# Start of each image in a two-layer Mamba and FFN kernel: order of the loads, engine of the column copies, queue of the first inputs

## The chip, the core and the metric

The kernel runs on one core of one Trainium2 chip. The time is that of the device, in microseconds; for the kernel before it is the median of three runs. The core has five engines that this text names: TensorE (PE in the profile, PEld its weight loads), VectorE (DVE), ScalarE (ACT), GpSimd (POOL) and SyncE (SP), which only issues transfers. Each engine works through its own instructions in order.

## The reference

The input x is two images of 96 channels and 128 by 128 pixels, fp32. Two layers are applied.

```python
x = x + L0_conv(ln_c(x))        # four Mamba scans, see below
t = tokens(x); t = t + ffn0(ln_t(t)); x = image(t)
x = x + conv3x3(ln_c(x))        # 3x3, 96 to 96 channels
t = tokens(x); t = t + ffn1(ln_t(t)); x = image(t)
```

`ln_c` is layer norm over the 96 channels of a pixel. `L0_conv` runs a Mamba block over four orders of the 16,384 pixels: by rows, by rows backwards, by columns, by columns backwards. Each block projects 96 to 2 x 192 channels, takes a causal convolution of four taps and SiLU, forms dt, B and C of 16 states, and scans:

```python
h = exp(dt * A) * h + dt * B * u      # 192 channels x 16 states, one step a pixel
y = sum_s(h * C) + D * u;  y = y * silu(z);  out = y @ outp_w.T
```

The four results are put back in image order, joined and projected to 96 channels. The FFN rounds its operands to an 8-bit float and its sums to fp16.

## The kernel before

An image is held in SBUF as one tile `acc` of 96 partitions by 16,384 pixels. Ahead of the images the constants are loaded (L51, helper `const`), and a block of preparation (L78 to L105) loads six weight tensors and forms four tables from them: `amat` (L81, L82), `dmat` (L88), `inx`, which merges the input projection with the convolution's taps (L95), and `gmat`, eight small matmuls and copies (L104, L105). Then for each of the two images three functions run one after another.

`normalize` (L149) reads the image in eight blocks of 2,048 pixels (L147; for the second image seven of them were read during the first image's FFN), takes the layer norm of 32 tiles of 512 pixels (L110 to L124), and stores the result to DRAM twice: by rows as `xnr` (L165) and by columns as `xnc`. For the second, eight staging tiles `stg` of 2,048 pixels (768 KB, three buffers) are filled from the strided view of `xn`, one half by VectorE and one half by ScalarE (L173), and each is stored (L177).

`mamba` (L179) handles the orders in two pairs: rows and columns forwards (pi = 0), then both backwards. A step is one tile of 512 pixels of a pair; there are 64 steps an image. A step's 384 channels lie in three groups of 128, and for each group the 16 states are scanned two at a time, so a step is 24 units, and an image 1,536. In a unit ScalarE makes the decay (L353), GpSimd multiplies B's broadcast rows (L345), VectorE scans (L357) and multiplies with C's rows (L445), and TensorE sums over the states (L361). Ahead of a step stands its prologue: it loads the normalized tile by rows (`xa`) and by columns (`xb`) (L218 for the first step of a pair, after two memsets of the edge at L217; L220 for the others), takes the convolution as matmuls (L204) for the groups in the order 1, 0, 2, with ScalarE emptying PSUM (L231), spreads the mixed group 1 over the partitions with two transfers (`xc<-mix`, L248), applies SiLU (L251), and makes the rows of B, C and dt (L258 to L305). The rows go to DRAM (`bcd`, L269) and are read back broadcast over the partitions (`row`, L341).

`ffn_and_conv` does the rest of the image, and stores it.

What sets the order: all five engines run in the order in which the program is written (`in_order`, L138). `together` (L126) interleaves generators: in each turn every stream makes one step, and stream r starts at turn r, so that layer norm's 32 tiles stand as a pipeline of five stages. A prologue's pieces carry a place (`at` in `prologue`), counted in units, at which they are issued; the first prologue of an image is issued at once. All transfers are issued by SP, in the written order; a transfer also waits for the eighth one before it, since eight semaphores are taken in turn. Pools are laid one behind another in SBUF and are freed as a stack, so the first tile of a new pool waits for those that lay in the same place.

Of the kernel before, what the change touches and what calls it, by code (L numbers as in the profile page):

```python
# [10 lines left out]
F32 = mybir.dt.float32  # L11
# [5 lines left out]
PSUM = bass.MemoryType.PSUM  # L17
# [24 lines left out]
def tile_metaformer(ctx: ExitStack, tc: tile.TileContext, a: dict, out: bass.AP):  # L42
    nc = tc.nc

    cpool = ctx.enter_context(tc.tile_pool(name="const", bufs=1))
    accp = ctx.enter_context(tc.tile_pool(name="accp", bufs=1))
    dpool = ctx.enter_context(tc.tile_pool(name="dram", bufs=2, space=DRAM))

    def const(name, shape):
        t = cpool.tile(list(shape), F32, name=name)  # L50
        nc.sync.dma_start(t, a[name])  # L51
        return t
# [7 lines left out]
    minus_one = cpool.tile([128, 1], F32, name="minus_one")  # L60
    nc.vector.memset(minus_one, -1.0)
    ident = const("ident", (128, 128))
    center = cpool.tile([C, C], F32, name="center")
    nc.vector.tensor_scalar_add(center, ident[0:C, 0:C], -1.0 / C)
    inz = const("inz", (C, 4, DI))
# [9 lines left out]
    dmat = cpool.tile([128, 2, NG, 128], F32, name="dmat")  # L75
    gmat = cpool.tile([128, 2, NG + 1, C], F32, name="gmat")
    inx = cpool.tile([C, 4, 4, DI], F32, name="inx")
    with tc.tile_pool(name="prep", bufs=1) as pp, tc.tile_pool(name="prep_ps", bufs=2, space=PSUM) as pps:  # L78
        alog = pp.tile([128, 2, NG, S], F32, name="alog")
        nc.sync.dma_start(alog, a["alog"])  # L80
        nc.scalar.activation(alog, alog, AF.Exp)  # L81
        nc.vector.tensor_scalar_mul(amat, alog, -1.0)  # L82

        dskip = pp.tile([128, 2, NG], F32, name="dskip")
        nc.sync.dma_start(dskip, a["dskip"])
        for pi in range(2):
            for g in range(NG):
                nc.vector.tensor_scalar_mul(dmat[:, pi, g, :], ident, dskip[:, pi, g : g + 1])  # L88

        inxw = pp.tile([C, 4, DI], F32, name="inxw")  # L90
        nc.sync.dma_start(inxw, a["inx"])
        taps = pp.tile([C, 4, 4, DI], F32, name="taps")
        nc.sync.dma_start(taps, a["taps"].broadcast_to((C, 4, 4, DI)))
        for d in range(4):
            nc.vector.tensor_tensor(inx[:, d], taps[:, d], inxw[:, d, None, :].broadcast_to((C, 4, DI)), ALU.mult)  # L95
        outx = pp.tile([C, 2, NG + 1, 128], F32, name="outx")
        nc.sync.dma_start(outx, a["outx"])
        fusew = pp.tile([C, 4, C], F32, name="fusew")
        nc.sync.dma_start(fusew, a["fusew"])
        for pi, pair in enumerate(PAIRS):  # L100

            for g in range(NG + 1):
                ps = pps.tile([128, C], F32, name="ps")
                nc.tensor.matmul(ps, outx[:, pi, g, :], fusew[:, pair[g // 2], :], start=True, stop=True)  # L104
                nc.vector.tensor_copy(gmat[:, pi, g, :], ps)  # L105

    def layernorm(x, eps, dst, wp, psp, bufs=2, **cast):

        xm = psp.tile([C, T], F32, name="xm", bufs=bufs)
        nc.tensor.matmul(xm, center, x, start=True, stop=True)  # L110
        yield
        sq = wp.tile([C, T], F32, name="sq")
        nc.scalar.activation(sq, xm, AF.Square)  # L113
        yield
        v = psp.tile([C, T], F32, name="v")
        nc.tensor.matmul(v, mean_w, sq, start=True, stop=True)  # L116
        yield
        rs = wp.tile([C, T], F32, name="rs")
        nc.scalar.activation(rs, v, AF.Ln, bias=eps)  # L119
        nc.scalar.activation(rs, rs, AF.Exp, scale=-0.5)  # L120
        yield
        if len(dst.shape) == 3:
            xm, rs = (t.rearrange("c (h w) -> c h w", w=W) for t in (xm, rs))
        nc.vector.tensor_tensor(dst, xm, rs, ALU.mult, **cast)  # L124

    def together(*streams):  # L126

        turn = 0
        streams, done = list(streams), object()
        while streams:  # L130
            left = []
            for at, g in streams:
                if turn < at or next(g, done) is not done:
                    left.append((at, g))
            streams = left
            turn += 1
# [6 lines left out]
    blk = 4 * T  # L143

    def read(b, acc, j):

        nc.sync.dma_start(acc[:, bass.ts(j, blk)], a["x"][b, :, bass.ts(j, blk)])  # L147

    def normalize(b, acc, xnr, xnc):  # L149

        with ExitStack() as st:
            pool = lambda n, bufs, **kw: st.enter_context(tc.tile_pool(name=n, bufs=bufs, **kw))
            full, wp, psp = pool("n1", 1), pool("n2", 3), pool("n_ps", 3, space=PSUM)
            in_order(st)
            nc.scalar.preload_act_table_set("natural_log_exp_and_others")
            xn = full.tile([C, L], F32, name="xn")
            for j in range(L // blk if b == 0 else 1):
                read(b, acc, j if b == 0 else L // blk - 1)

            def one(r):  # L160
                sl = bass.ts(r, T)
                yield from layernorm(acc[:, sl], eps_c[0:C, 0:1], xn[:, sl], wp, psp, 5)
                if (r + 1) % 4 == 0:
                    sl = bass.ts(r // 4, blk)
                    nc.sync.dma_start(xnr[:, sl], xn[:, sl])  # L165

            together(*((r, one(r)) for r in range(NT)))
            cols = xn.rearrange("c (h w) -> c w h", w=W)
            for j in range(L // blk):
                stg = wp.tile([C, blk], F32, name="stg")  # L170
                half = blk // W // 2
                for i, eng in enumerate((nc.vector.tensor_copy, nc.scalar.copy)):
                    eng(  # L173
                        stg[:, i * half * W : (i + 1) * half * W].rearrange("c (w h) -> c w h", h=W),
                        cols[:, j * 2 * half + i * half : j * 2 * half + (i + 1) * half, :],
                    )
                nc.sync.dma_start(xnc[:, bass.ts(j, blk)], stg)  # L177

    def mamba(acc, xnr, xnc):  # L179

        with ExitStack() as st:
            pool = lambda n, bufs, **kw: st.enter_context(tc.tile_pool(name=n, bufs=bufs, **kw))
            io, one, two, gen = pool("io", 2), pool("one", 1), pool("two", 2), pool("gen", 4)
            ps_w, ps_y, ps_m = (pool(n, k, space=PSUM) for n, k in (("ps_w", 3), ("ps_y", 1), ("ps_m", 1)))
            rows_d = pool("rows_d", 3, space=DRAM)

# [20 lines left out]
            def prologue(pi, i, d):  # L207

                rev = pi == 1
                lo = L - (i + 1) * T if rev else i * T  # L210
                src = []

                def load():
                    for n, dram in (("xa", xnr), ("xb", xnc)):
                        t = io.tile([C, T + 3], F32, name=n)
                        if i == 0:
                            nc.gpsimd.memset(t[:, T : T + 3] if rev else t[:, 0:3], 0.0)  # L217
                            nc.sync.dma_start(t[:, 0:T] if rev else t[:, 3 : T + 3], dram[:, lo : lo + T])  # L218
# [20 lines left out]
                    nc.scalar.copy(mixed("sz") if g == 1 else d["sz"][:, g, :], d["ps"])  # L239

                def mixed(name):
                    d["mix", name] = one.tile([128, T], F32, name="mix")
                    return d["mix", name]

                def mix(name):
# [227 lines left out]
            for k in range(total + 6):  # L473
# [22 lines left out]
    def ffn_and_conv(b, acc):  # L496

        with ExitStack() as st:
# [32 lines left out]
            def ffn(n, r):  # L531
# [64 lines left out]
    acc = accp.tile([C, L], F32, name="acc")  # L596
# [77 lines left out]
```

## Time and profile before

| | us |
|---|---|
| median of three runs | 12174.19 |
| the three runs | 12160.50 to 12199.53 |
| the profiled execution | 12198.56 |
| its span | 12196.8 |
| busy VectorE, GpSimd | 10962.5, 9908.7 |
| busy TensorE, ScalarE | 10601.0, 8585.5 |

The profile is that of one execution. Its page gives, by engine, the busy time and the busy share in 40 equal slices of the span, and groups of instructions by line, with their mean duration in nanoseconds and the idle time of the engine just before them. A line of the timeline has the start and the duration in us, the engine, the line of the code, the operation, what it writes and reads, the number of instructions that were merged into the line, and in brackets how long the engine had been idle and what released it. A table of stretches gives the busy time of PE, PEld, DVE, ACT and POOL in each, with the number of instructions, then TensorE's granted clock, the share of the transfer engines and GB/s. "To landing" is the time from a transfer's issue to its last byte.

### The profile page before, as it was taken

Reading aid. Unit: us, or ns where it says so; the run is one execution under the profiler, and the core shown is the slowest. Engines: PE = TensorE matmul, PEld = TensorE weight load, DVE = VectorE, ACT = ScalarE, POOL = GpSimd, SP = SyncE. Lnnn points to the kernel's source line nnn. Section 1 sums busy time; section 2 is a strip of 40 time slices with the busy share of each in tenths; the row PEclk is TensorE's granted clock in tenths of the full one; section 3 lists DMA queues with packets and bytes.
Section 4 is the critical chain, followed back from the end, with each engine's and each line's share of the span. In section 5 each row is a group of like instructions: output and inputs, shape, how many; then the busy total and the mean of one; then the engine's idle time right before and its main releaser. Section 6 shows DMA issues by size and latency. Waiting matters only on the chain. (4 is left out here: it accounts for less than half of the span.)

```text
span 12196.8 us, 95712 instructions
## 1 busy us (share of the span) xinstructions
PE 10601.0 (87%) x24208; PEld 4012.8 (33%) x24208; DVE 10962.5 (90%) x10624; ACT 8585.5 (70%) x15110; POOL 9908.7 (81%) x5336
## 2 busy tenths in 40 slices
PE   7888888888888888888978888888888888888889
PEld 2333333333333333333323333333333333333333
DVE  6999999999999999995469999999999999999954
ACT  6777777777777777775577777777777777777655
POOL 5998999999998989891159989999989999988811
PEclk9999999999999999999989999999999999999999
DMA  7887888788877878781068888888878878878700
GB/s 250 309 319 302 307 319 313 309 318 312 318 310 306 319 305 310 308 317 47 26 242 307 308 317 312 314 318 313 313 307 308 321 308 316 314 305 309 304 32 13
DMA packets 539169, 3417.07 MB, mean 280 GB/s; under 512 B 67276, under 2 KB 68396, under 8 KB 140696
## 3 DMA queue, kind: packets, MB, share of 16 engines
q1 hardware_dynamic: 538616, 3410.94, 72.9%
q8 instruction: 195, 3.19, 0.1%
q14 instruction: 358, 2.93, 0.1%
HBM read 3289.04 MB, written 54.53 MB: 274 GB/s over the span
## 5 line engine op out<-in xcount | busy, mean ns | idle before, releaser
L345 POOL TENSOR_TENSOR row<-dtu,row 128x2048 f32<-128x2048 f32 x1536 | 6949.9, 4525 | 820.8 <-DMA row<-bcd 658.5
L357 DVE TENSOR_TENSOR_SCAN da<-da,row 128x512 f32<-128x512 f32 x5632 | 6650.2, 1215 | 509.8 <-ACT da L353 187.3
L361 PE MATMUL y<-row,ident 128*128 128x512 f32 x12288 | 5957.9, 618 | 1130.5 <-DVE row L445 1125.7
L353 ACT ACTIVATE da<-dt,amat 128x512 f32<-128x512 f32 x6144 | 4250.4, 692 | 278.7 <-DVE row L357 92.0
L361 PEld LDWEIGHTS y<-row,ident 128*128 128x128 f32 x12288 | 2268.5, 194 | 4643.0 <-issue 2296.4
L445 DVE TENSOR_TENSOR row<-da,row 128x1024 f32<-128x1024 f32 x2816 | 3395.8, 1206 | 1.0 <-DMA row<-bcd 0.9
L446 ACT COPY hst<-da 128x2 f32<-128x2 f32 x2816 | 434.7, 154 | 1423.8 <-DVE row L445 1412.4
L204 PE MATMUL misc<-xa,inx 96*64 96x512 f32 (+1 forms) x2048 | 963.6, 614 | 131.3 <-DMA xa<-xnr 108.0
L204 PE MATMUL misc<-xb,inx 96*64 96x512 f32 (+1 forms) x2048 | 962.3, 613 | 1.9 <-ACT xc L231 1.6
L568 POOL TENSOR_TENSOR acc<-acc,y 96x512 f32<-96x512 f32 x128 | 147.4, 1152 | 987.1 <-DVE y L567 987.1
L357 DVE TENSOR_TENSOR_SCAN row<-da,row 128x512 f32<-128x512 f32 x512 | 616.9, 1205 | 0.0
L364 POOL TENSOR_TENSOR row<-row,row 128x1024 f32<-128x1024 f32 x256 | 602.8, 2355 | 7.1 <-DVE row L357 6.1
L580 PE MATMUL pc<-pad,kw 96*96 96x512 f32 x1152 | 566.7, 593 | 0.0
L452 PE MATMUL y<-xc,dmat 128*128 128x512 f32 x768 | 428.9, 640 | 145.2 <-DVE sz L368 145.2
L295 POOL TENSOR_TENSOR q<-e,q 128x512 f32<-128x512 f32 x384 | 487.5, 1270 | 71.5 <-ACT q L292 71.5
L204 PEld LDWEIGHTS misc<-xa,inx 96*64 96x64 f32 (+1 forms) x2048 | 329.7, 166 | 650.6 <-issue 444.9
L231 ACT ACTIVATE xc<-misc,convb 128x512 f32<-128x512 f32 x256 | 175.8, 687 | 519.7 <-PE misc L204 519.7
L301 POOL TENSOR_TENSOR dt<-dt,ln 128x512 f32<-128x512 f32 x384 | 487.1, 1269 | 30.1
L298 POOL TENSOR_TENSOR ln<-ln,q 128x512 f32<-128x512 f32 x384 | 487.2, 1269 | 20.1
L305 POOL TENSOR_TENSOR dtu<-dt,xc 128x512 f32<-128x512 f32 x384 | 487.1, 1269 | 10.2
L378 PE MATMUL misc<-sz,gmat 128*96 128x512 f32 x1024 | 483.6, 594 | 0.0
L124 DVE TENSOR_TENSOR xq<-xm,rs 96x512 fp8e5<-96x512 f32 x128 | 87.9, 687 | 388.0 <-ACT rs L120 387.9
(81 smaller groups left out, 9340.4 us busy)
## 6 DMA issues: line engine op xcount, KB each, us to landing
row<-bcd SPq DMA_DIRECT2D x3072, 1024.0 KB, 7.1
xc<-mix SPq DMA_DIRECT2D x256, 128.0 KB, 5.3
sz<-mix SPq DMA_DIRECT2D x256, 128.0 KB, 5.4
xa<-xnr SPq DMA_DIRECT2D x124, 193.1 KB, 5.2
xb<-xnc SPq DMA_DIRECT2D x124, 193.1 KB, 5.5
bcd<-rows SPq DMA_DIRECT2D x128, 128.0 KB, 6.7
acc<-in_x_dram SPq DMA_DIRECT2D x16, 768.0 KB, 8.6
xnr<-xn SPq DMA_DIRECT2D x16, 768.0 KB, 4.3
```

The lines of the kernel that those rows point to most:

```text
L204: nc.tensor.matmul(ps[rows, :], w(PAIRS[pi][d], k, lo, hi), src[d][:, k : k + T], **se)
L295: nc.gpsimd.tensor_tensor(d["q"], d["e"], d["q"], ALU.subtract)
L298: nc.gpsimd.tensor_tensor(d["ln"], d["ln"], d["q"], ALU.add)
L301: nc.gpsimd.tensor_tensor(d["dt"][g], d["dt"][g], d["ln"], ALU.add)
L305: nc.gpsimd.tensor_tensor(dtu, d["dt"][g], d["xc"][:, g, :], ALU.mult)
L345: nc.gpsimd.tensor_tensor(b, d["dtu"][g][:, None, :].broadcast_to((128, 4, T)), b, ALU.mult)
L353: nc.scalar.activation(da[:, j, :], d["dt"][g], AF.Exp, scale=amat[:, pi, g, s + j : s + j + 1])
L357: nc.vector.tensor_tensor_scan(h[:, j, :], da[:, j, :], b[:, j, :], 0.0, ALU.mult, ALU.add)
L361: nc.tensor.matmul(y, ident, c[:, j, :], start=False, stop=s + j == S - 1)
L364: nc.gpsimd.tensor_tensor(c, h, c, ALU.mult)
L445: nc.vector.tensor_tensor(c, h, c, ALU.mult)
L580: nc.tensor.matmul(pc, kw[:, t, :], rows, start=t == 0, stop=t == 8)
```

## The change

Three things are done.

First, the eight reads of the first image are written right behind the load of `ident`, ahead of the other constants and the weights. The preparation becomes a generator `prep` that is one more stream of `together` in the first image's layer norm. Its six loads are issued in turn 0; in turn 18 it forms `amat`, in the two turns after that `dmat`, in four more `inx`, and then a product of `gmat` a turn, copied in the next. Its PSUM pool has one buffer for two, layer norm's `v` two for three.

Second, the columns are copied by VectorE alone, in 16 parts of eight columns (1,024 pixels, 384 KB) with three buffers, in a pool of their own that is opened after layer norm; each part is stored by itself.

Third, the first two inputs of the forward pair are issued on GpSimd's queue, each behind its memset, for SP's. The backward pair's stay on SP. The pools of `normalize` and `mamba` are laid out in another order: layer norm's scratch first, then `xn`; `io` (xa, xb), `gen`, `one`, a pool of its own for `mix`, `two`.

```diff
+    acc = accp.tile([C, L], F32, name="acc")
+    blk = 4 * T
+    def read(b, acc, j):
+        nc.sync.dma_start(acc[:, bass.ts(j, blk)], a["x"][b, :, bass.ts(j, blk)])
+    for j in range(L // blk):
+        read(0, acc, j)
     center = cpool.tile([C, C], F32, name="center")
...
-    with tc.tile_pool(name="prep", bufs=1) as pp, tc.tile_pool(name="prep_ps", bufs=2, space=PSUM) as pps:
-        alog = pp.tile([128, 2, NG, S], F32, name="alog")
-        nc.sync.dma_start(alog, a["alog"])
+    def prep(st):
+        pp = st.enter_context(tc.tile_pool(name="prep", bufs=1))
+        pps = st.enter_context(tc.tile_pool(name="prep_ps", bufs=1, space=PSUM))
...
+        alog, dskip = load("alog", (128, 2, NG, S)), load("dskip", (128, 2, NG))
+        outx, fusew = load("outx", (C, 2, NG + 1, 128)), load("fusew", (C, 4, C))
+        inxw, taps = load("inx", (C, 4, DI)), load("taps", (C, 4, 4, DI), spread=True)
+        for _ in range(18):
+            yield
         nc.scalar.activation(alog, alog, AF.Exp)
         nc.vector.tensor_scalar_mul(amat, alog, -1.0)
...
         for pi in range(2):
+            yield
             for g in range(NG):
                 nc.vector.tensor_scalar_mul(dmat[:, pi, g, :], ident, dskip[:, pi, g : g + 1])
...
         for d in range(4):
+            yield
             nc.vector.tensor_tensor(inx[:, d], taps[:, d], inxw[:, d, None, :].broadcast_to((C, 4, DI)), ALU.mult)
...
                 nc.tensor.matmul(ps, outx[:, pi, g, :], fusew[:, pair[g // 2], :], start=True, stop=True)
+                yield
                 nc.vector.tensor_copy(gmat[:, pi, g, :], ps)
...
-            full, wp, psp = pool("n1", 1), pool("n2", 3), pool("n_ps", 3, space=PSUM)
+            wp, psp = pool("n2", 3), pool("n_ps", 2, space=PSUM)
             in_order(st)
             nc.scalar.preload_act_table_set("natural_log_exp_and_others")
+            full = pool("n1", 1)
             xn = full.tile([C, L], F32, name="xn")
-            for j in range(L // blk if b == 0 else 1):
-                read(b, acc, j if b == 0 else L // blk - 1)
+            if b > 0:
+                read(b, acc, L // blk - 1)
...
-            together(*((r, one(r)) for r in range(NT)))
+            streams = [(r, one(r)) for r in range(NT)]
+            with ExitStack() as weights:
+                together(*streams, *([(0, prep(weights))] if b == 0 else []))
+            stg = pool("n3", 3)
             cols = xn.rearrange("c (h w) -> c w h", w=W)
-            for j in range(L // blk):
-                stg = wp.tile([C, blk], F32, name="stg")
...
+            part = 8
+            for j in range(W // part):
+                t = stg.tile([C, part, W], F32, name="stg")
+                nc.vector.tensor_copy(t, cols[:, bass.ts(j, part), :])
+                nc.sync.dma_start(xnc[:, bass.ts(j, part * W)], t.rearrange("c w h -> c (w h)"))
...
-            io, one, two, gen = pool("io", 2), pool("one", 1), pool("two", 2), pool("gen", 4)
+            io, gen, one, mixp, two = (pool(*p) for p in (("io", 2), ("gen", 4), ("one", 1), ("mixp", 1), ("two", 2)))
...
                             nc.gpsimd.memset(t[:, T : T + 3] if rev else t[:, 0:3], 0.0)
-                            nc.sync.dma_start(t[:, 0:T] if rev else t[:, 3 : T + 3], dram[:, lo : lo + T])
+                            queue = nc.sync if rev else nc.gpsimd
+                            queue.dma_start(t[:, 0:T] if rev else t[:, 3 : T + 3], dram[:, lo : lo + T])
...
-                    d["mix", name] = one.tile([128, T], F32, name="mix")
+                    d["mix", name] = mixp.tile([128, T], F32, name="mix")
```

More of the change, by code (lines that the diff above doesn't have):

```diff
@@ L77, in tile_metaformer, with load @@
     inx = cpool.tile([C, 4, 4, DI], F32, name="inx")
-    with tc.tile_pool(name="prep", bufs=1) as pp, tc.tile_pool(name="prep_ps", bufs=2, space=PSUM) as pps:
-        alog = pp.tile([128, 2, NG, S], F32, name="alog")
-        nc.sync.dma_start(alog, a["alog"])
+    def prep(st):
+        pp = st.enter_context(tc.tile_pool(name="prep", bufs=1))
+        pps = st.enter_context(tc.tile_pool(name="prep_ps", bufs=1, space=PSUM))
+        def load(name, shape, **kw):
+            t = pp.tile(list(shape), F32, name=name)
+            nc.sync.dma_start(t, a[name].broadcast_to(shape) if kw else a[name])
+            return t
+        alog, dskip = load("alog", (128, 2, NG, S)), load("dskip", (128, 2, NG))
[3 more added lines that the diff above has]
+            yield
         nc.scalar.activation(alog, alog, AF.Exp)
         nc.vector.tensor_scalar_mul(amat, alog, -1.0)
-        dskip = pp.tile([128, 2, NG], F32, name="dskip")
-        nc.sync.dma_start(dskip, a["dskip"])
         for pi in range(2):
+            yield
             for g in range(NG):
                 nc.vector.tensor_scalar_mul(dmat[:, pi, g, :], ident, dskip[:, pi, g : g + 1])
[L90 to L93, printed above, removed]
         for d in range(4):
+            yield
             nc.vector.tensor_tensor(inx[:, d], taps[:, d], inxw[:, d, None, :].broadcast_to((C, 4, DI)), ALU.mult)
[L96 to L99, printed above, removed]
         for pi, pair in enumerate(PAIRS):
@@ L141, in in_order @@
         st.enter_context(tc.manual_schedule(engines={et.Activation, et.DVE, et.Pool, et.PE, et.SP}))
-    blk = 4 * T
-    def read(b, acc, j):
-        nc.sync.dma_start(acc[:, bass.ts(j, blk)], a["x"][b, :, bass.ts(j, blk)])
     def normalize(b, acc, xnr, xnc):
@@ L165, in one @@
                     nc.sync.dma_start(xnr[:, sl], xn[:, sl])
-            together(*((r, one(r)) for r in range(NT)))
+            streams = [(r, one(r)) for r in range(NT)]
+            with ExitStack() as weights:
+                together(*streams, *([(0, prep(weights))] if b == 0 else []))
+            stg = pool("n3", 3)
             cols = xn.rearrange("c (h w) -> c w h", w=W)
-            for j in range(L // blk):
-                stg = wp.tile([C, blk], F32, name="stg")
[L171 to L177, printed above, removed]
+            part = 8
[3 more added lines that the diff above has]
+                nc.sync.dma_start(xnc[:, bass.ts(j, part * W)], t.rearrange("c w h -> c (w h)"))
     def mamba(acc, xnr, xnc):
@@ L594, in ffn_and_conv @@
                 together(*((at, f(r - lag)) for lag, at, f in stages if 0 <= r - lag < NT))
-    acc = accp.tile([C, L], F32, name="acc")
     for b in range(NB):
```

## The prediction, written before the result was known

> **What bounds the kernel now.** I read the page first, then a table of four long stretches, then the timeline of the two places that the change touches.
>
> ```profile
> DVE   6999999999999999995469999999999999999954
> ...
> L357 DVE TENSOR_TENSOR_SCAN da<-da,row 128x512 f32<-128x512 f32 x5632 | 6650.2, 1215 | 509.8 <-ACT da L353 187.3
> ```
> ```profile
> 3000.00:4000.00 1000.00, 878.05 (x1979) 330.56 (x1978) 963.93 (x870) 724.90 (x1284) 908.81 (x489) 0.98 0.81 312
> ```
> In the scan loop VectorE (third busy figure) works 964 of 1000 us. The change leaves that loop's instructions alone: the built programs hold the same ones in the same order on every engine. So the only time at stake lies where VectorE is not yet scanning: the first slice (6 of 10) and the same place in image 2, just after the 4 and 5. The loop hands any earlier start on to the end, since each image is serial: normalize, mamba, ffn.
>
> ```profile
> 6.77 8.79 SPq L147 DMA_DIRECT2D acc<-in_x_dram  x8
> ...
> 20.82 3.73 PE L110 MATMUL xm<-acc,center 96*96 96x512 f32 x4 [0.35 <-DVE gmat L105]
> 22.88 0.59 ACT L113 ACTIVATE sq<-xm 96x512 f32<-96x512 f32 x1 [16.01 <-PE xm L110]
> ```
> Timeline of the start: layer norm's first matmul comes at 20.82, released by the last weight product (gmat); the image is asked for only at 6.77.
>
> ```profile
> 80.38 0.69 DVE L124 TENSOR_TENSOR xn<-xm,rs 96x512 f32<-96x512 f32 x1 [0.61 <-ACT rs L120]
> 81.10 5.58 ACT L173 COPY stg<-xn 96x1024 f32<-96x1024 f32 x3 [0.75 <-DVE xn L124]
> 81.11 2.90 DVE L173 COPY stg<-xn 96x1024 f32<-96x1024 f32 x3
> ...
> 88.36 1.02 DVE L173 COPY stg<-xn 96x1024 f32<-96x1024 f32 x1 [4.35 <-DMA xnc<-stg]
> 98.57 1.92 ACT L173 COPY stg<-xn 96x1024 f32<-96x1024 f32 x1 [0.63 <-DMA xnc<-stg]
> 100.55 0.10 POOL L217 MEMSET xa<- 96x3 f32 x1 [100.09 <-ACT stg L173]
> 100.87 1.27 SPq L218 DMA_DIRECT2D xa<-xnr  x1
> 102.19 1.80 SPq L218 DMA_DIRECT2D xb<-xnc  x1
> 107.38 1.09 PE L204 MATMUL misc<-xa,inx 96*64 96x512 f32 x1 [28.41 <-DMA xa<-xnr]
> 113.88 1.19 SPq L248 DMA_DIRECT2D xc<-mix  x2
> 122.83 1.28 ACT L251 ACT_TABLE_LOAD   x1
> 151.40 3.61 DVE L357 TENSOR_TENSOR_SCAN da<-da,row 128x512 f32<-128x512 f32 x3 [51.78 <-POOL row L345]
> ```
> From layer norm to the first scan everything is in series. Layer norm ends at 81.07 (call such an end E), column copies end at 100.5, the first inputs xa, xb arrive at 107.4, three convolutions fill 15.4 us, SiLU's table load starts at 122.83 (E+41.8), the first scan 28.6 later. Image 2: E is 6166.67, the table load 6208.65 (E+42.0).
>
> ```profile
> L173 ACT COPY stg<-xn x8: 1915/1922/1936, 81.1 to 98.6; 96x1024 f32<-96x1024 f32 x8
> L173 DVE COPY stg<-xn x8: 1022/1028/1036, 81.1 to 98.6; 96x1024 f32<-96x1024 f32 x8
> ...
> DMA to landing us min/median/max: 5.2/5.5/6.7
> ```
> The view of tile stg: the copies wait for their stores. Their starts (91.02, 93.49, 96.02, 98.57) stand 2.5 us apart, 768 KB each: some 310 GB/s, so the transfers set the pace and a copy has slack.
>
> [...]
>
> **Part 1, image ahead of weights.** The eight reads move from place 14 on SP's queue to place 2, so from 6.77 to about 1.2. A 288 KB read (inz) landed in 3.1 us at that hour; 480 KB more at the start's 250 GB/s is 1.9: the first block lands at about 1.2+5.1 = 6.3. center is ready at 2.9. The first xm thus comes at 6.3, not 20.82: -14.5. Later blocks (3.1 us each) outrun four tiles of 1.72. Bounds: -16 (4.8) to -12 (8.8).
>
> What moves on SP: inz to fuseb and the six prep loads go behind the reads, and each issue waits for the transfer eight before it. The reads end near 28, taps (7.9 us in its row) lands near 39. The first taps product stands in turn 21, at 6.3+5.4+18x1.717 = 42.6: hidden, with 4 us to spare. The first three xnr stores queue behind taps until about 31 and catch up by layer norm's end; nobody reads them before.
>
> **Part 2, products between tiles.** A tile takes 1.717 us, all of it ScalarE (0.57+0.67+0.63, overlapping a little). alog's exp is ScalarE's: +0.28. VectorE has 1.03 free a turn: three dmat 0.63, one inx 0.95, one gmat copy 0.26 all fit. TensorE's 0.86 a turn takes a 96-column product of about 0.3. v's PSUM buffers fall from 3 to 2: v of tile r needs the Ln of tile r-2, which stands a turn earlier on ScalarE: nothing. Total +0.3; upper bound, if 15 turns lose 0.5 each, +7.5; below nothing is excluded, since ScalarE sets the turn. **Start: -14.2.**
>
> **Part 3, copies on VectorE, pools laid out anew, inputs on GpSimd's queue** (once for each image). ScalarE loses eight 1.92 us copies, VectorE has 16 of 1.03 in 16 parts of 384 KB with three buffers. The pools now lie so that xa and xb are behind layer norm's scratch and wait only for its end (E), not for the last copy; xc, mix, sz lie beyond the staging buffers. The built program confirms it: xa waits for xnr's first store, xb for xnc's first part, both long before the copies end. Two arms follow.
>
> Copies: the last xnr block (4.3 alone) goes first, part 1 lands at E+4.3+1.25 = 5.6. A 192 KB store (out) lands in 2.1 us; 192 KB more at 310 is 0.6, so a part lands in 2.7; with copy and wakes 4.0 for three, 1.33 a part (bandwidth alone: 1.25). The 16th copy starts at 5.6+12x1.33 = 21.6, ends at 22.6, say 23.3 with xa and xb's 384 KB among them. That is 4 us later than before's 19.4. Then xc's two mix DMAs, which stand on SP behind all 16 stores: 0.6 each to issue, 2.4 to land when the queue is empty, 5.3 in the loop; I take 3.3 from the second issue: E+27.
>
> Inputs: xb may go at E+5.6. [...]as VectorE idles 0.3 of each 1.33 I take 2. Landing 4 (4.1 median, 2.8 to 5.3 for xb in this stage): E+11.5. The convolutions[...] take their 15.4: E+27, while ScalarE, free of copies, empties them. GpSimd has nothing queued behind the two DMAs until q (L295).
>
> SiLU's load needs both arms: E+27 against E+41.8 and 42.0: -14.8 and -15.0. What is late next, from SiLU to the scan, is unchanged. One wait is new there: rows (ScalarE, with the whole dt chain behind it) now lies where staging was and waits for the last stores, landed by E+26 and thus before it.
>
> **Sum.** -14.2-14.8-15.0 = -44. The profiled execution took 12198.6 (span 12196.8 and 1.8 around it), 24 above the median; no term depends on that, so I take 44 from the median: 12174-44 = **12130**. The loop is costed at nothing: its tiles have new addresses, but the same instructions, queues and buffer counts.
>
> **Rivals.** (A) GpSimd is starved: [...]xb lands at E+27, the convolutions end at E+42: part 3 gives nothing, 12174-14 = 12160. For it: [...]VectorE copies 77% of the time. Against: [...]VectorE waits after each copy for a store. (B) Partly so, or part 2 stretches: xb at E+15 to E+20, or 7 us in layer norm: -24 to -37, about 12143. (C) Slower: the three smaller buffers make the column copies latency-bound. SiLU then starts at E+10.6+12p, p the time of a part: 14.2+2x(41.9-10.6-12p) = 0 at p = 3.2, so it turns at 3.2 us a part, slower by 0.3% at 4.7; at p = 5 the end is +43, 12217. For it: the copies waited for stores before too. Against: a part would have to land in 13 us, and 768 KB landed in 5.5 with others in flight. (D) The change doesn't do what it says: excluded by the built order for the reads and the queue.
>
> **Chances.** 0.3% (36.5 us, about what a measurement can tell) is the bound. Forecast 0.60, its own range 12108 to 12138 (part 1's -16 to -12, xb 3 us either way, 8 us of the median's own scatter, whose runs span 39); A 0.14; B 0.20; C and an unforeseen loss in the loop (15 ns in each of 3072 units would eat all) 0.06. The range runs through B to A: 12108 to 12164. Faster by over 0.3%: most of the forecast, a little of B, 0.56; slower 0.05; within, 0.39.
>
> **What would show it.** First xm near 6.3 and layer norm's end near 67; parts 1.3 us apart; xa's memset at E, not behind the copies; xb landing near E+11.5; SiLU's table load 27 after E in both images; first scan near 122.5. Wrong if xb's matmuls wait beyond the last copy (A), if tiles in the product turns take over 1.8 (B), if parts take over 3 (C), or if VectorE's busy share in the stretch 3000 to 4000 leaves 96%.

## The result and the profile after

The kernel after took 12104.61 us (median of 7 runs, 12084.5 to 12140.8) against 12174.85 for the kernel before, run beside it (7 runs, 12160.5 to 12199.5): ratio 0.9944, 95% interval 0.9927 to 0.996. That is 70 us less; the prediction said 44 less, 12130, with 12108 as the lower end. The profiled execution of after took 12104.61 (span 12102.8), that of before 12198.56 (span 12196.8): 94.0 between the spans.

From the page of the kernel after: VectorE's 40 slices, its scans, and the convolutions' matmuls.

```profile
DVE  7999999999999999995479999999999999999954
...
L367 DVE TENSOR_TENSOR_SCAN da<-da,row 128x512 f32<-128x512 f32 x5632 | 6647.6, 1215 | 420.4 <-ACT hst L456 158.6
L213 PE MATMUL misc<-xa,inx 96*64 96x512 f32 (+1 forms) x2048 | 950.7, 607 | 60.3 <-DMA xa<-xnr 44.2
```

The first digit is 7 instead of 6: the start is shorter. But the scans, whose instructions did not change, also have less idle time ahead of them: 420.4 us, where the page of before has 509.8. And the matmuls on xa, deep in the loop, waited 44.2 us for the transfer of xa; in before it was 108.0:

```profile
L204 PE MATMUL misc<-xa,inx 96*64 96x512 f32 (+1 forms) x2048 | 963.6, 614 | 131.3 <-DMA xa<-xnr 108.0
```

The stretch 3000 to 4000 of after, with the columns as before (VectorE third), does not show it: VectorE's share is what was forecast, 96%. The prediction had named that share as its sign for the loop, and one stretch was too coarse for it:

```profile
3000.00:4000.00 1000.00, 875.39 (x1966) 331.13 (x1965) 960.74 (x868) 723.37 (x1283) 904.66 (x488) 0.98 0.80 313
```

The timeline of after, from the first xm over layer norm's end (E, here 69.59) to the first scan:

```profile
7.01 3.70 PE L124 MATMUL xm<-acc,center 96*96 96x512 f32 x4 [7.01 <-DMA acc<-in_x_dram]
...
68.90 0.69 DVE L138 TENSOR_TENSOR xn<-xm,rs 96x512 f32<-96x512 f32 x1 [0.55 <-ACT rs L134]
69.62 2.90 DVE L184 COPY stg<-xn 96x1024 f32<-96x1024 f32 x3
69.71 0.97 POOL L226 MEMSET xa<- 96x3 f32 x1 [69.25 <-DVE xn L138]
70.21 1.49 POOL L228 DMA_DIRECT2D xa<-xnr  x1
75.94 0.94 POOL L228 DMA_DIRECT2D xb<-xnc  x1 [3.39 <-DMA xnc<-stg]
80.18 1.08 PE L213 MATMUL misc<-xb,inx 96*64 96x512 f32 x1 [1.99 <-DMA xb<-xnc]
93.85 1.04 DVE L184 COPY stg<-xn 96x1024 f32<-96x1024 f32 x1 [0.18 <-DMA xnc<-stg]
95.32 2.15 SPq L258 DMA_DIRECT2D xc<-mix  x2
99.40 1.28 ACT L261 ACT_TABLE_LOAD   x1 [3.27 <-DMA xc<-mix]
127.58 3.61 DVE L367 TENSOR_TENSOR_SCAN da<-da,row 128x512 f32<-128x512 f32 x3 [32.68 <-POOL row L355]
```

Here is the whole difference of the two spans, cut at these events (first scan to last scan for a loop):

| stretch | before | after | difference | predicted |
|---|---|---|---|---|
| to the first xm | 20.82 | 7.01 | -13.8 | -14.5 |
| layer norm, image 1 | 60.25 | 62.58 | +2.3 | +0.3 |
| E to SiLU's load, image 1 | 41.8 | 29.8 | -12.0 | -14.8 |
| SiLU's load to first scan, image 1 | 28.6 | 28.2 | -0.4 | 0 |
| loop, image 1 | 5380.3 | 5349.8 | -30.5 | 0 |
| loop end to E of image 2 | 635.0 | 633.2 | -1.8 | 0 |
| E to first scan, image 2 | 68.15 | 58.86 | -9.3 | -15.0 |
| loop, image 2 | 5382.2 | 5355.5 | -26.7 | 0 |
| to the end | 579.8 | 577.9 | -1.9 | 0 |

The starts gave 33 of the 94, the loops 57. The median step of a loop is 83.13 us in both kernels; only the number of longer steps differs. The convolutions of a step have their place in unit 1, on the inputs xa and xb that were asked for in unit -2. Call a step late when TensorE stood over 1 us waiting for them. Of the 122 steps that lie inside a direction, 29 are late in before and 12 in after. Late ones took 86.85 and 86.93 us on the mean, the others 83.37 and 83.39. Summed over 83.13, the late steps cost 107.9 and 45.6 us: 62 of difference; the other steps cost 22 and 29, so that 55 of the loops' 57 are found.

Two steps of the kernel before, an undisturbed one (first scan at 1157.8) and a late one (at 1070.3):

```profile
1155.87 0.42 SPq L220 DMA_DIRECT2D xa<-xnr  x1
1162.12 0.64 PE L204 MATMUL misc<-xa,inx 96*64 96x512 f32 x1
1165.83 0.69 ACT L231 ACTIVATE mix<-misc,convb 128x512 f32<-128x512 f32 x1 [0.61 <-PE misc L204]
```
```profile
1068.29 0.42 SPq L220 DMA_DIRECT2D xa<-xnr  x1
1076.68 1.38 PE L204 MATMUL misc<-xa,inx 96*64 96x512 f32 x2 [2.06 <-DMA xa<-xnr]
1078.70 1.06 PE L204 MATMUL misc<-xa,inx 96*64 96x512 f32 x1
1080.97 0.59 PE L204 MATMUL misc<-xa,inx 96*64 96x512 f32 x1
1082.68 0.69 ACT L231 ACTIVATE mix<-misc,convb 128x512 f32<-128x512 f32 x1 [5.04 <-PE misc L204]
1084.84 1.23 DVE L357 TENSOR_TENSOR_SCAN da<-da,row 128x512 f32<-128x512 f32 x1 [1.42 <-ACT da L353]
```

Both issues come 2.0 us before the first scan of their step. In the first the convolution begins 6.25 us after the issue, in the second 8.4 us after it, 2.06 of them idle. TensorE's granted clock, 1.00 until then, is 0.50 in the records from 1077.26 to 1080.67, and most matmuls of the convolution take 1.06 us there, where 0.59 is usual; so the mix comes 14.4 us after the issue instead of 10.0. In ScalarE's written order, mix stands ahead of the next decay (da), and the scan waits for that decay.

The reason that xa was late can be read from the 16 completions that the trace has of each transfer. In this late step fifteen of xa's had come 3.7 us after the step's first scan, the last at 6.3. In step 4 of before it was 3.3 and 6.5, and around the late step the last completion of xb and of four row transfers also came 2.3 to 3.2 us behind the fifteenth. The last of xa's came at 1076.55, the first matmul began at 1076.68. Which of the 16 it is, and why it is late, stays open.

### The profile page after: what moved, and what is told of

It reads as the page before. It is cut to its first block, busy times and chain, and to the rows that moved or that the text cites. A ratio compares the mean times of both kernels' runs of the same rounds, so it can differ in the third digit from the quotient of the medians.

```text
span 12102.8 us, 95756 instructions
## 1 busy us (share of the span) xinstructions
PE 10567.0 (87%) x24208; PEld 3990.8 (33%) x24208; DVE 10976.2 (91%) x10640; ACT 8560.2 (71%) x15094; POOL 9914.8 (82%) x5340
## 5 line engine op out<-in xcount | busy, mean ns | idle before, releaser
L367 DVE TENSOR_TENSOR_SCAN da<-da,row 128x512 f32<-128x512 f32 x5632 | 6647.6, 1215 | 420.4 <-ACT hst L456 158.6
L213 PE MATMUL misc<-xa,inx 96*64 96x512 f32 (+1 forms) x2048 | 950.7, 607 | 60.3 <-DMA xa<-xnr 44.2
```

What stands on the lines that cost most here:

```text
L213: nc.tensor.matmul(ps[rows, :], w(PAIRS[pi][d], k, lo, hi), src[d][:, k : k + T], **se)
L367: nc.vector.tensor_tensor_scan(h[:, j, :], da[:, j, :], b[:, j, :], 0.0, ALU.mult, ALU.add)
```

## The experiments

The theory, **late inputs**: the loop's gain is that fewer steps get xa and xb late. The rivals: the **addresses** of the loop's tiles, which part 3 changed, made it faster; it was **chance** in the runs compared; or late inputs are only a **sign** of slow transfers, which stall VectorE by another way. For the start, the prediction's own rivals are tried. Ratios and their 95% intervals are to the kernel before on the same chip. The kernels with early inputs ran on three chips (early_before and early_after on one; early_sp, early_mix and early_split on a second; lead3, own_turn, four_bufs and parts4 on a third), and none of them on two. Their loops, each by itself, agree within 5 us over the three chips, so differences of 9 us and more between them are read, with the events of the traces beside them, and smaller ones are not.

**early_before and early_after.** Both kernels, with the inputs asked for six units earlier:

```
-                at = [(-2, 1, load), (2, 1, partial(mix, "xc")), ...
+                at = [(-8, 1, load), (2, 1, partial(mix, "xc")), ...
...
-                if u == nu - 2:
+                if u == nu - 8:
```

> The kernel before, with each step's xa and xb asked for in unit -8 instead of unit -2, six units (some 21 us) ahead. Theory 'late inputs': the waits of TensorE over 1 us for xa go from 30 steps to under 3, nearly every step takes the median 83.1 us, a loop comes to about 64 x 83.1 = 5320 to 5330 instead of 5381, and the time falls by 100 to 120 us to some 12055 to 12075. Rival (late rows, not late inputs, hold VectorE up; the inputs are only late with them): the waits on xa go, but the time stays within 20 us of 12175.

> The kernel after with the same edit. Theory 'late inputs': the 13 late steps go too, the loops fall from 5350 and 5356 to 5320 to 5330, the time from 12105 to some 12040 to 12055; the distance to the kernel before with the same edit is then what the starts alone gave, about 33 us. Rival: 12105 as it was, and the distance stays 70.

Measured: 12076.6 (5 runs within 4 us; ratio 0.994, 0.9928 to 0.9952) and 12042.7 (5 runs within 7 us; 0.9911, 0.99 to 0.9923). No step but the first of an image is late, and the four loops take 5318.3 to 5321.7 us. The page of early_after:

```profile
L213 PE MATMUL misc<-xa,inx 96*64 96x512 f32 (+1 forms) x2048 | 939.7, 601 | 24.9 <-DMA xa<-xnr 17.1
```

What is left of the 44.2 us lies at the starts. Row transfers are no better than before: of those that could be timed, 13.0% and 14.6% had their last part over 1.6 us behind the eighth, against 12.9% (before) and 8.7% (after). So rows with a late part cost nothing that shows here, and the late inputs cost the 73 and 83 us that are gained over the means of after and before below. Between the two early kernels lie **33.9 us**: that is what the change itself gives when inputs aren't late. The scatter of the runs, 39 and 56 us in the first comparison, falls to 4 and 7: the rest was late steps.

**lead3.** One unit of lead, on the kernel after: `(-3, 1, load)` and `nu - 3`.

> The kernel after, each step's xa and xb asked for in unit -3 instead of -2 (or -8): one unit, 3.46 us, more. The late inputs of the traces landed 7.2 to 9.8 us after their issue, where the convolutions need them some 6.2 after it; with 9.7 to go by, nearly all come in time: 12043 to 12052, 0 to 3 late steps, scatter under 12 us. If more than the lateness of single transfers is behind it, the gain is in proportion to the lead (1 unit of 6): some 12095 to 12102.

Measured: 12041.73 (4 runs; 0.9896, 0.9878 to 0.9913), no late step. The issue moved from 2.0 to 8.1 us before the first scan, more than a unit, since on SP's queue it now stands ahead of the two row loads of unit -2; three such loads hold SP for 6.45 us in the kernel after, ahead of one step's xa (957.49).

**lead1 and lead0.** Later instead of earlier, on the kernel after: `(-1, 1, load)` with `nu - 1`, and `(0, 0, load)`.

> The kernel after, each step's xa and xb asked for in unit -1 instead of -2: 3.46 us later. The traces give 6.2 us from issue to the first convolution's place in unit -2, and 5.1 to 5.5 us to landing; now the convolutions' place comes 2.8 us after the issue, so every step is late, by 2.4 us at least. A late step (TensorE waiting over 1 us) took 86.9 us in the traces against 83.1. Theory 'late inputs': every step takes some 86.5 to 88, the loops 126 x 3.4 to 4.9 = 430 to 610 us more than without a late step (12043): 12470 to 12650. If a late step is a sign of slow transfers and not the cause of the stall: 12105 plus at most 50.

Measured: 12126.0 (11 runs; 0.9971, 0.996 to 0.9981). The expectation was wrong, and for a reason to remember: there is no row load on SP's queue between units -2 and -1, so the queue's order, and the issue at -2.0, stayed. The built program is the kernel after, but for the place of two memsets on GpSimd in one step. Its runs count as runs of after below.

> The kernel after, each step's xa and xb asked for at the start of unit 0, behind the row loads of units -2 and 0 on SP's queue. (The edit to unit -1 had moved nothing: SP's queue holds no row load between the two places, and the built program was the kernel after again.) The issue comes some 0.4 us after the step's first scan, 2.4 later than in the kernel after; the inputs land near 5.7 where the convolution's place is 4.3, so every step is late by some 1.4 us. By the 905 steps of the traces so far, a gap of 1.0 to 1.5 us costs a step 1.9 us: 126 x 1.9 = 240 over the kernel with early inputs, and the steps with a slow transfer cost more than now: 12300 to 12450. If lateness is a sign of slow transfers and not the cause of the stall: 12115, plus at most 50.

Measured: 12406.48 (4 runs; 1.0214, 1.0196 to 1.0232). The issue is at +0.5, 119 of 122 steps are late and take 86.1 us on the mean.

```profile
L213 PE MATMUL misc<-xa,inx 96*64 96x512 f32 (+1 forms) x2048 | 996.8, 632 | 280.3 <-DMA xa<-xnr 236.2
```

The sign theory is out: the same transfers, asked for 2.5 us later, cost 290 us (over 12116, the mean of all runs of after), where it allowed 50.

**loop_layout, twice.** The kernel before with mamba's pools in the order of after, which gives the loop's tiles the addresses that they have in after (mix gets a pool of its own here too). xa and xb have the same addresses in all three kernels:

```
-            io, one, two, gen = pool("io", 2), pool("one", 1), pool("two", 2), pool("gen", 4)
+            io, gen, one, mixp, two = (pool(*p) for p in (("io", 2), ("gen", 4), ("one", 1), ("mixp", 1), ("two", 2)))
...
-                    d["mix", name] = one.tile([128, T], F32, name="mix")
+                    d["mix", name] = mixp.tile([128, T], F32, name="mix")
```

> The kernel before, with only the order of the five tile pools of mamba as in the kernel after, so that every tile of the scan loop has the address it has there; the start is the old one. Theory 'late inputs' (the loop's gain is that fewer steps get their xa and xb late, and this has nothing to do with addresses): no change, 12165 to 12185 us, some 25 to 30 of 126 steps with TensorE waiting over 1 us for xa. Rival 'addresses' (the new places of the tiles in SBUF are what made the loop shorter): the loop's share of the gain, 70-33 = 37 us, so 12138, and some 13 late steps.

> The kernel before with the pools of mamba in the order of after, once more: -7.5 us (-16 to +2) at the first time. If its addresses make late inputs rarer, by some 13 us, it is 5 to 20 us under the kernel before again; without such an effect, within 5 us of it on the mean of both times.

Measured: 12148.9 (14 runs; 0.9994, 0.9985 to 1.0004), then 12141.51 (22 runs; 0.9987, 0.9979 to 0.9994). On the means that is 7.5 and 15.5 us below before. The 37 us of the rival are excluded. The first interval includes no effect, the second doesn't, and by what was written beforehand (5 to 20 us under before a second time) a small part, some 8 to 15 us, goes with the layout. Its profiles have 13 and 16 late steps.

**after_again and after_third.**

> The kernel after, unchanged, once more beside the kernel before. The starts alone are worth 33 to 34 us (sum of the start phases in the two traces, and the distance of the two kernels with early inputs). Theory 'chance': what the first comparison showed beyond them, 70 - 33 = 37 us, was scatter of late inputs; the distance now is 25 to 45 us. Rival 'something in the kernel after makes late inputs rarer': the distance stays at 60 to 75.

> The kernel after once more, for the question whether late inputs are rarer in it than in the kernel before. From the runs so far: before (45 runs) 12160 mean, 83 over the same kernel with early inputs; after (13 runs) 12112 mean, 70 over its own. Starts alone: 34 to 35 us between them. 'No difference but chance': the distance here is 25 to 45. 'Rarer': 50 to 70.

Measured: 12114.79 (6 runs; 0.9962, 0.9948 to 0.9975), then 12109.86 (6 runs; 0.9962, 0.9949 to 0.9975). By the means the distance was 69 in the first comparison, then 46, 48, and 36 in lead1's. Over all, 93 runs of before have a mean of 12159.9 and 30 of after 12115.6: **44 us**, of which 34 are the starts and some 10 late steps. So the first comparison showed some 25 us more than all together. The excess lies in its kernel before: mean 12180.1, where the five later comparisons have 12152 to 12172, and its after, 12111.3, is like the later ones (12110 to 12123). One run of before scatters by 15.6 us (standard deviation), so a mean of seven by 6; 20 above the mean of all is more than chance from run to run gives. The comparisons ran at different times and on several chips, and no run shows whether one of these makes late parts more frequent. What the traces show is that the late steps follow the late parts: in the eight profiles with inputs at -2.0, those with 8.7 to 9.1% of their row loads late (last part over 1.6 us behind the eighth) have 11 to 14 late steps, those with 10.0 to 11.0% have 16 to 18, and the first profile of before has 12.9% and 29. It took 12198.6, as much as the longest of its runs.

So of the first 70 us, 34 are the starts, some 25 belong to the occasion, with its cause open, and some 10 are left. The layout may explain these, since loop_layout gained as much. How an address would change a transfer's lateness no run shows.

**read_ahead.** Parts 1 and 2 alone: `read`, `prep` and the streams of after, with the copies, queue and pools of before.

> Parts 1 and 2 alone: the image read ahead and the weights' products between layer norm's tiles; the column copies (2048 columns at a time, half on VectorE and half on ScalarE), the first inputs on SP's queue and mamba's pools are those of the kernel before. By the trace of the kernel after: first xm at 7.0, layer norm ends at 69.6, 11.5 earlier, so 12163; the predicted step was -14.2, 12160. Layer norm takes 62.6 (not 60.3), if the products' turns stretch it. The loop is left at what it was before (5380) if its gain came with part 3's addresses, and falls by some 20 us an image if it came by chance or with the earlier start.

Measured: 12150.11 (13 runs; 0.9995, 0.9987 to 1.0003). First xm at 7.14, E at 68.73, SiLU's load at E+42.5 and E+43.5. The total can't tell 12 us from the scatter; the events can, and part 3's gain is absent, as it should be.

**early_sp, early_mix, early_split**: the parts of part 3, on early_after, where the runs of a kernel agree within 7 us.

```
-                            queue = nc.sync if rev else nc.gpsimd
+                            queue = nc.sync
```

> The kernel after with inputs asked for in unit -8 (12042.7, runs within 7 us of each other), and the first xa and xb of each image back on SP's queue, behind all 16 column stores. The prediction's rival A in its form: xb is issued near E+25 instead of E+6.4, its matmuls begin near E+30, three convolutions of 15.4 end near E+45 and SiLU's table load comes at E+45 to 46 instead of E+30: 15 us an image, so 12073. If GpSimd's queue were worth little (the copies' arm sets the end by itself): within 5 us of 12043.

Measured: 12070.06 (4 runs; 0.9927, 0.9913 to 0.9941), 27.4 more. SiLU's load is at E+45.8 and E+45.5. Timeline of early_sp (E at 68.7):

```profile
93.98 0.90 SPq L228 DMA_DIRECT2D xb<-xnc  x1
98.01 1.09 PE L213 MATMUL misc<-xa,inx 96*64 96x512 f32 x1 [31.55 <-DMA xa<-xnr]
...
114.52 1.28 ACT L261 ACT_TABLE_LOAD   x1
```

Without GpSimd's queue part 3 is a loss: E+45.8 is later than the E+41.8 of before.

```
-                        nc.sync.dma_start(d[name][k:128:2, 1, :], d["mix", name][64 * k : 64 * k + 64, :])
+                        (nc.gpsimd if pi == 0 and i == 0 and name == "xc" else nc.sync).dma_start(d[name][k:128:2, 1, :], d["mix", name][64 * k : 64 * k + 64, :])
```

> The kernel after with early inputs, and xc's two mix DMAs of each image's first step on GpSimd's queue instead of SP's, where they stand behind the 16 column stores. If that place is what sets SiLU (issued at E+25.7, landing at E+29.8), SiLU's load now waits for the last convolution, which ended at E+26.5: -2.5 to -3.5 an image, so 12036 to 12038. If the transfers themselves are late (DMA is busy with the stores until E+28), no gain: 12041 to 12044. [...]

Measured: 12033.64 (4 runs; 0.9898, 0.9884 to 0.9912), 9.1 less, a little more than expected; the two SiLU loads come 3.9 and 2.8 us earlier, the first scans 5.3 and 4.0. Timeline of early_mix (E at 68.6):

```profile
86.00 1.77 POOL L258 DMA_DIRECT2D xc<-mix  x2 [9.92 <-DMA xnc<-stg]
...
94.69 1.28 ACT L261 ACT_TABLE_LOAD   x1
```

The load follows the last convolution's result directly, at E+26.1: the inputs' arm, as the prediction had it.

```
-                nc.vector.tensor_copy(t, cols[:, bass.ts(j, part), :])
+                (nc.scalar.copy if j % 2 else nc.vector.tensor_copy)(t, cols[:, bass.ts(j, part), :])
```

> The kernel after with early inputs, and every other column copy on ScalarE (which part 3 of the change took them off); queue, buffers and pools as they are. ScalarE's copies stand ahead of its reading of the convolutions, so the first convolution's result waits for the last ScalarE copy, near E+24, and two more convolutions of about 5 us follow, with their result: SiLU's load near E+36 instead of E+30: +6 an image, 12055. If ScalarE's copies made the parts quicker than 1.5 us: less, down to 12045.

Measured: 12051.72 (4 runs; 0.9913, 0.9896 to 0.9929), 9.0 more; SiLU's load at E+33.7 and E+34.7. So VectorE's taking all copies is worth some 4.5 us an image (3.7 and 4.7 at SiLU's load).

**own_turn.** On early_mix, a turn for each weight product and another for its copy; `others` holds the dskip and tap products, which go into the turns between:

```
+                yield
                 ps = pps.tile([128, C], F32, name="ps")
                 nc.tensor.matmul(ps, outx[:, pi, g, :], fusew[:, pair[g // 2], :], start=True, stop=True)
+                if others:
+                    others.pop(0)()
                 yield
                 nc.vector.tensor_copy(gmat[:, pi, g, :], ps)
```

> The kernel with early inputs and the first mix DMAs on GpSimd's queue (12033.6), and each of the eight weight products with a turn of its own: product in one turn, gmat copy in the next, the dskip and tap products in the turns between. If the turns of 1.91 us came from the next product waiting on TensorE for the copy of the one before, with layer norm's v matmul behind it, no turn waits now: layer norm falls from 62.6 to 60.3 to 60.7 us and the time by 2, to some 12031 to 12032. If they came from the one PSUM buffer fewer for v, or from more work on VectorE, layer norm stays at 62 to 63.

Measured: 12031.71 (4 runs; 0.9887, 0.9872 to 0.9901), but layer norm took 61.4 us in both kernels: the theory of the copy fell, though the time came where it had put it. The 1.9 us to early_mix, on another chip, are no gain that the runs show. Turns with a product still took 1.91 us, those without 1.72, alternating. TensorE's timeline in the kernel after shows why:

```profile
60.35 1.02 PE L124 MATMUL xm<-acc,center 96*96 96x512 f32 x2
61.21 0.36 PE L117 MATMUL ps<-fusew,outx 96*128 96x96 f32 x2
61.41 1.02 PE L130 MATMUL v<-sq,mean_w 96*96 96x512 f32 x2
62.27 1.02 PE L124 MATMUL xm<-acc,center 96*96 96x512 f32 x2
```

xm holds TensorE from 60.35 to 61.21 and v from 61.41 to 62.27: 0.86 each, 1.72 a turn without a gap. A turn fills TensorE as it fills ScalarE (1.717 us), and a product adds its 0.19 wherever it stands.

**four_bufs and parts4**, for the prediction's rival C, on early_after: four staging buffers instead of three, and parts of four columns.

```
-            wp, psp = pool("n2", 3), pool("n_ps", 2, space=PSUM)
+            wp, psp = pool("n2", 2), pool("n_ps", 2, space=PSUM)
...
-            stg = pool("n3", 3)
+            stg = pool("n3", 4)
```

> The kernel after with early inputs (12042.7), with four staging buffers instead of three (layer norm's sq and rs give up one of three each, which their turns allow). If the pace of a part, 1.5 us where 1.33 was predicted, comes from waiting for a store to land before a buffer is free, a part goes to about 1.25, the last copy ends near E+22, and SiLU's load then waits for the convolutions: E+26.5 instead of E+29.8: -6 for both images, 12037. If it is the bandwidth of the stores, the pace stays and so does the time: 12041 to 12044.

Measured: 12068.27 (4 runs; 0.9917, 0.9902 to 0.9931), 25.6 more, and not for the buffers. With sq and rs in two buffers layer norm's scratch ended 128 bytes before the pool of xa and xb does, and that end lay on xn. The inputs again waited for the last column copy, from the timeline of four_bufs (E at 69.5):

```profile
90.81 0.10 POOL L226 MEMSET xa<- 96x3 f32 x1 [90.35 <-DMA xnc<-stg]
```

That is the old wait, brought back by 128 bytes. The pace did quicken: the last copy ended at E+21.1, where early_sp, with three buffers and no inputs among the copies either, has E+24.4. So waiting for one of three buffers to be stored, not the bandwidth, held the pace.

```
-            part = 8
+            part = 4
```

> The kernel after with early inputs, column copies in 32 parts of four columns (192 KB) with the same three buffers. The prediction's rival C in the flesh: a store of 192 KB takes some 2.6 us to land, copy and waits 1.1 more, so three in flight give 1.24 us a part, 2.5 for eight columns instead of 1.5; the last copy ends near E+41, SiLU's load comes near E+46 instead of E+30: +16 an image, 12075. If bandwidth sets the pace, 1.5 for eight columns stays: 12043 to 12046.

Measured: 12054.7 (4 runs; 0.9906, 0.9891 to 0.9921), 12.0 more. A part took 1.0 us at the median, 1.19 on the mean, so 2.0 to 2.4 for eight columns, and the last copy ended at E+39.8. But SiLU's load came at E+25.7: in the built order of SP's queue the mix DMAs now stood between the stores, after 9 and 12 of the 32, and the price appeared after SiLU (first scan at E+63.8). The mechanism of rival C is real; the expectation had over-estimated its size, and the expected path, mix behind all stores, did not hold.

## Why the prediction was wrong

**The step that failed** is the last sentence of the sum: "The loop is costed at nothing: its tiles have new addresses, but the same instructions, queues and buffer counts." The same instructions did take less, 57 us in the profiles and 36 by the first medians (70 less the 34 of the starts). A step's time depends on whether a transfer lands in the 6.2 us until its use, and one in ten to one in four did not. The profile of before had it: 108.0 us of TensorE's idle time by xa, and 187.3 of the scans' by da. The prediction showed the second of these lines and took from it only that VectorE was busy. From such a wait it should have taken a range for the loop, up to the 108.0 us that TensorE waited, or at least asked whether the runs' scatter of 39 us was made there.

**The first xm** came at 7.01, not 6.3: -13.8, right within its bounds of -16 to -12.

**Layer norm** was mis-sized: "ScalarE sets the turn" and "TensorE's 0.86 a turn takes a 96-column product" are wrong. xm and v together hold TensorE 1.72 a turn, and the turns with a product took 1.91, over the 1.8 that the prediction had named as its sign for rival B. Measured +2.3: 1.4 from seven product turns that stretch by 0.19, 0.2 from the turn with alog's exp, and 0.8 from the second tile (2.49 us after the first here, 1.72 to 2.39 in the other profiles with this start).

**The inputs' arm** held: xb issued at E+6.4 (5.6 predicted), its first matmul at E+10.6 (11.5), last convolution ended at E+26.5 (27). The 2 us put down for xb's issue were the author's estimate, as the trace of before has no transfer on GpSimd's queue; the issue took 0.94. Rival A, which had no trace behind it either, is excluded by the timeline, since xb arrived while the copies ran: GpSimd's issue of xb ended 0.11 us after the copy in hand, and 12 copies were still to come (last section).

**The copies' arm** was mis-sized. From the view of tile stg of the kernel after:

```profile
DVE stg L184: 18.2, 20
...
DMA to landing us min/median/max: 2.8/3.6/5.7
```

VectorE waited 18.2 us in 20 places for a store to land. A landing takes 3.6 us at the median where 2.7 was worked out, a part 1.5 us, not 1.33, and the last copy ended at E+25.3 (23.3), the mix was issued at E+25.7, and SiLU's load came at E+29.8 and E+30.3 instead of E+27. So 12.0 and 11.7 were gained instead of 14.8 and 15.0; early_mix took that back, 6.7 us at SiLU and 9.1 in the time.

**The sum of the starts** was 33 in the profiles and 34 between the early kernels, against 44: 0.7 at the first xm, 2.0 in layer norm, 2.8 and 3.3 before SiLU, and 2.0 between SiLU and the scans. There image 2 lost 2.4: its first row landed 7.9 us after the issue, 6.0 in before, and TensorE's products ahead of it took 0.5 more. Over all runs the distance is 44, 34 from the starts and some 10 from fewer late steps, which may go with the layout. That the forecast's 44 equals this is luck: the starts came 10 short, and the loop, put at nothing, gave 10. The first comparison's 70 has some 25 us in it that later ones did not show, and the 8 us of scatter allowed in the range did not cover them.

## What to carry to other kernels

Give a transfer that feeds a chain the slack of its late cases, not of its median: here 5.2 us was the median landing, 6.2 the slack, and 7 to 10 the late ones, and moving the request two places up the queue, into a buffer that was already free, gained 73 us, more than the change under study (44). Place it by the order of its queue, since a new place in the program that passes nothing on the queue moves nothing. And where a kernel scatters by 50 us, find what scatters before comparing versions: with the late steps gone, runs agreed within 7 us and terms of 9 us could be told apart. The fastest versions made here, early_mix at 12033.64 and own_turn at 12031.71, have early inputs and the first mix on GpSimd's queue.

## What the runs showed of the hardware that was not expected

- Of the 16 parts of a transfer, the last landed up to 3.2 us after the other fifteen. In every profile, 9 to 15% of the 1 MB row loads had their last part over 1.6 us behind the eighth, and in 67 and 72% of these (before and after) the last alone was over 1 us behind the fifteenth. Around the late step above, six transfers issued within 10 us (xa, xb and four row loads) shared it, with 2.3 to 3.2 us between the two.
- A late input cost a step more where a lower clock followed it. Over 976 steps of eight profiles, a gap of 2.0 to 2.5 us ahead of the convolutions cost a step 2.9 us when the records show TensorE's clock at 1.00 (11 steps) and 4.6 when they show 0.50 after the gap (19 steps).
- GpSimd beside VectorE's copies was held up by the copy in hand, and no longer: in after the issue of xa ended at 71.70, 0.11 us behind the second of three copies that followed one another directly. From the timelines of after, parts4 (smaller copies) and early_split (here ScalarE alone copies at that moment):

```profile
75.74 1.03 DVE L184 COPY stg<-xn 96x1024 f32<-96x1024 f32 x1 [3.22 <-DMA xnc<-stg]
75.94 0.94 POOL L228 DMA_DIRECT2D xb<-xnc  x1 [3.39 <-DMA xnc<-stg]
```
```profile
75.38 0.73 DVE L184 COPY stg<-xn 96x512 f32<-96x512 f32 x1 [3.74 <-DMA xnc<-stg]
75.58 0.65 POOL L228 DMA_DIRECT2D xb<-xnc  x1 [3.91 <-DMA xnc<-stg]
```
```profile
75.20 0.52 POOL L228 DMA_DIRECT2D xb<-xnc  x1 [4.41 <-DMA xnc<-stg]
```

In the first two the issue ends 0.11 to 0.12 us after the copy, as do the issues of xa; a memset of three columns took 0.97 us and ended 0.03 after a copy, and took 0.10 with none in its way. Beside copies of 1.03 us the issue of xb took 0.94 us, where without one it took 0.52: 0.42 more.
